# One more row block gathered in the first layer, one-hots made two batches ahead, idle products in a shorter opening, and last matrices in another PSUM pool

## The chip, the core and the metric

The kernel runs on one core of a Trainium2 chip. The core has five engines with queues of their own: TensorE (PE, matrix products), VectorE (DVE), ScalarE (ACT), GpSimd (POOL) and SyncE (SP, which here only issues transfers). They go in step only through semaphores. The metric is the device time of one execution in microseconds, as the median of several runs.

## What is computed

A graph of 6250 nodes with 256 channels and 100000 edges goes through four layers. Each layer adds to every node the sum over its incoming edges and then runs a small network of three matrices:

```python
def agg(h):
    return jax.ops.segment_sum(h[src], dst, num_segments=N)
h = max(layernorm(x), 0)
for l in range(3):
    g = h + agg(h)
    g = relu(g @ W1s[l] + b1s[l]); g = relu(g @ W2s[l] + b2s[l]); h = g @ W3s[l] + b3s[l]
g = h + agg(h)
g = relu(g @ cW1 + cb1); g = relu(g @ cW2 + cb2)      # 64 channels
out = x + g @ cW3 + cb3
```

The edges come sorted by destination. All numbers are float32.

## The kernel before

The nodes are cut into 49 row blocks of 128 nodes. The first matrix of each layer is applied before the sum, so that a layer's input is kept in SBUF as `XY` (49 blocks, each with a high and a low part of 256 columns). For a row block the sum over edges is made in one of two ways.

- **By a product.** For the block an adjacency matrix of 128 columns by 49 x 128 rows with the counts of edges is built once, in the first layer, as bytes. A product with all of `XY` (49 matmuls of 128x512, line 1642 in the first layer, line 1720 in panels later) then gives the sums. The counts are cast to float on ACT or DVE (lines 1602 and 1618) ahead of the product.
- **By a gather.** POOL issues 17 indirect DMAs for the block (line 1427). Each brings 128 source rows into one of 24 buffers named `rows`. When the block's *visit* comes, PE sums those rows with one-hot matrices (line 1466, 46 matmul records in the trace) into `sums`, and DVE adds the result to the block's own row (`u`, lines 1486 and 1495).

In the first layer (called layer 0 in the code) 26 blocks are products and 23 are gathered. In the three layers behind it 20, 20 and 18 are gathered.

**Building the matrices** (`build`, lines 1092 to 1130) fills layer 0 beside the products. It goes in batches of four sub-lists of edges, and a batch is two *steps*. For a batch DVE makes two one-hot tensors, `lo` (`low_hot`) and `hi` (`high_hot`, both line 1073); each is a tile with two buffers. A step is two matmuls (line 1114) into a PSUM bank `bp`, and a copy to bytes into `at` (ACT in odd steps, line 1122, DVE in even ones, line 1124). Sixteen steps are one block. A finished block gets the identity added (line 1128) and is stored by SP (line 1129) for the later layers. 31 blocks are built in all, since five are wanted only later. The order of the blocks is the list `made`.

**The opening.** Nothing can be multiplied before the first matrix is there. So `PRE` = 12 open steps of the outer clock `now` run two build steps each with no product beside them. Then the products start.

**What sets the order.** Every instruction is recorded in one Python program, and each engine carries out its own in that order. The outer clock `now` counts units of four product matmuls. In each unit `tick` runs what is due (`later`, `job`), then some build steps run up to `goals`, then `prepare` casts counts three units ahead, and then come the products. A second clock, `clock`, adds a fixed cost for each piece of PE work (`passed`) and stands for PE's time. From it `Gathered` sets the rate of the gathers: `pace` is the layer's modelled time divided by the number of its gathers. Each gather waits for the PE instruction at which the modelled time reaches it (`after(got, ...)`), and a visit comes when the modelled time says that its rows are there.

**The three dense matrices** of finished blocks (`mlp`) run in two later pieces, `seconds` and `thirds`, in PSUM tiles `ps` of a pool of two banks, `ps_m`. The products of the later layers use a pool of four banks, `ps_a`, under the name `agg`. At the end of the last layer the last panel and block 48 run in a hurry through `mlp`.

Of the kernel before, what the change touches and what calls it, by code (L numbers as in the profile page):

```python
# [8 lines left out]
F32 = mybir.dt.float32  # L9
# [8 lines left out]
P = 128  # L18
# [378 lines left out]
def sorted_edges(  # L397
# [77 lines left out]

    teams = [(18, 2), (20, 4), (24, 4), (28, 4), (32, 4), (36, 4), (40, 2), (42, 2)]
    made = [b + i for b, n in teams for i in range(n)]
    for i in range(panels[-1][1]):
        made.insert((4, 9, 14, 19)[i], panels[-1][0] + i)
    made.insert(25, 17)  # L480
# [520 lines left out]
    with tc.manual_schedule():  # L1001
# [90 lines left out]
        def build(hots, ats, ps_b):  # L1092
# [3 lines left out]
            pair(hots, 0)  # L1096
            low_hot(hots, 0)
            high_hot(hots, 0)
            step = 0
            for k, (s, q0) in enumerate(batches):  # L1100
# [6 lines left out]
                for q in range(0, BATCH, 2):  # L1107
                    if q == 0:
                        low_hot(hots, k + 1)
                    elif q == 2:  # L1110
                        high_hot(hots, k + 1)
                    bp = ps_b.tile([P, W], F32, name="bp")
# [8 lines left out]
                    if step % 2 or step <= 2 * PRE:  # L1121
                        nc.scalar.copy(o, v)  # L1122
                    else:
                        nc.vector.tensor_copy(o, v)  # L1124
                    if half and q0 + q + 2 == GSUB:
                        p, i = place_of[b]
                        own = at[:, b, :]
                        nc.vector.tensor_tensor(own, own, ident, OP.add)
                        nc.sync.dma_start(out=mats[p][:, :, i, :],
                                          in_=at.rearrange("p (k h) d -> p k (h d)", h=CH))  # L1130
# [66 lines left out]

        used, kept, wanted, lent = set(), set(), [], [0, 0]
        BACK = 3

# [49 lines left out]
        def mlp(l, b0, n, h1, hurry, far):  # L1250
# [7 lines left out]
            h2 = []  # L1258

            def second(i):  # L1260
                if i == 0:
                    h2.append(work.tile([P, KC, W], F32, name="h2"))
                ps = ps_m.tile([P, W], F32, name="ps")
                if twin:
# [17 lines left out]
            def halves():  # L1282
                m, w3 = n // 2, weights[l][1]
                pss = [ps_m.tile([P, W], F32, name="ps") for _ in range(2)]
                for q in range(m):
# [36 lines left out]
            def third(i):  # L1322
                m = min(2, n - i)
                w3 = weights[l][1]
                ps = ps_m.tile([P, W], F32, name="ps")
                for q in range(m):
# [32 lines left out]
            def seconds():  # L1359
                passed(BURST)  # L1360
                for i in range(-(-mid // P)):
                    second(i)
# [15 lines left out]
        class Gathered:  # L1378
# [30 lines left out]
            def begin(self):  # L1409
                self.one_hots(0)  # L1410
                self.end = begun[self.l] + work_of(self.l) - TAIL[self.l]
                self.pace = (self.end - clock[0] - MARGIN) / self.upto[-1]
                self.lead = MARGIN + self.upto[1] * self.pace
                self.first = clock[0] + self.lead
# [118 lines left out]

        EARLY = 8
        PRE = (GSUB + EARLY) // 2
# [130 lines left out]
        def product_of_team(b0, n, ps_a, beside, hurry):  # L1666
            us, h1 = [], []

            def turn(i, two):
                if not h1:  # L1670
                    h1.append(work.tile([P, KC, W], F32, name="h1", bufs=2) if hurry else
                              ats.tile([P, KC, W], F32, name="h1", bufs=1))
# [75 lines left out]
        with tc.tile_pool(name="hots", bufs=1) as hots, tc.tile_pool(  # L1748
# [9 lines left out]
            layers[0].send(8)  # L1758
            beside = build(hots, ats, ps_b)
            while now[0] < PRE:  # L1760
                for _ in range(2):
                    next(beside)
                    built[0] += 1
                tick(layers[0])
                layers[0].advance()
# [77 lines left out]
```

## Time and profile before

| | us |
|---|---|
| median of 3 runs | 2105.08 (2103.89 to 2105.66) |
| the profiled execution's own time | 2104.15 |
| its span, first to last instruction | 2102.4 |
| first build matmul | 116.58 |
| first product | 128.34 |
| last visit of layer 0 begins | 670.07 |
| first product of the next layer | 688.08 |
| PE busy | 2031.7 (97%) |
| POOL busy | 1441.1 (69%) |
| DVE busy | 933.8 (44%) |
| ACT busy | 879.7 (42%) |

Times inside the execution are counted from the span's start. In a row of the timeline stand the start, the length, the engine, the source line, the operation, the tile written and those read, and in brackets the idle time ahead of it with what ended that. "x4" is the number of instructions in the row. In a row of groups the number behind the bar is the busy time and the mean of one in nanoseconds. Matmuls overlap in the records: a row's length is longer than its distance to the next row, so rates of PE are read from start to start.

### The profile page before, as it was taken

The numbers are of one execution on the slowest core, as the hardware profiler recorded it, in microseconds if no ns is written. First come the engines' busy times: TensorE is split into PE (matmuls) and PEld (weight loads), VectorE is DVE, ScalarE is ACT, GpSimd is POOL, SyncE is SP. The second block draws the span as 40 slices with busy tenths as digits, with TensorE's granted clock in tenths as the row PEclk, the third lists the DMA queues.
The fourth block names the chain that finished last, engine by engine and source line by source line (L and its number), as shares of the span: only waits on it lengthen the run. The fifth ranks groups of instructions, "written<-read, shape, count | busy, mean of one in ns | idle before, by whom it ended". The sixth has DMA issues, their size and how long they took to land. (4 is left out here: it accounts for less than half of the span.)

```text
span 2102.4 us, 33308 instructions
## 1 busy us (share of the span) xinstructions
PE 2031.7 (97%) x12117; PEld 1501.4 (71%) x12117; DVE 933.8 (44%) x2108; ACT 879.7 (42%) x1799; POOL 1441.1 (69%) x1450
## 2 busy tenths in 40 slices
PE   6889999999999999999999999999999999999997
PEld 4667666666667777777777777777777777777775
DVE  5987767767673422222233322222224333333333
ACT  5866656556555523322333432323333433323331
POOL 3747777777774377777777377777777377777773
PEclk9999999999999999999999999999999999999999
DMA  5544545545554654545556555555456455656554
GB/s 166 171 136 137 158 150 154 157 150 153 155 153 145 212 163 146 169 152 179 155 174 196 186 165 149 172 159 179 147 171 202 161 179 156 196 174 206 169 171 129
DMA packets 184324, 346.92 MB, mean 165 GB/s; under 512 B 32030, under 2 KB 118080, under 8 KB 184150
## 3 DMA queue, kind: packets, MB, share of 16 engines
q0 software_dynamic: 68144, 183.13, 29.9%
q1 hardware_dynamic: 114078, 159.72, 23.1%
q8 instruction: 97, 1.59, 0.3%
q10 hardware_dynamic: 1928, 1.85, 0.3%
q14 instruction: 77, 0.63, 0.1%
HBM read 286.50 MB, written 58.07 MB: 164 GB/s over the span
## 5 line engine op out<-in xcount | busy, mean ns | idle before, releaser
L1427 POOL DMA_INDIRECT rows<-table,idx x1377 | 1381.2, 1003 | 587.5 <-issue 225.4
L1720 PE MATMUL agg<-a,XY 128*128 128x512 f32 x4116 | 976.6, 394 | 1.9 <-DVE clT L1654 1.9
L1720 PEld LDWEIGHTS agg<-a,XY 128*128 128x128 f32 x4116 | 765.2, 188 | 190.1 <-issue 32.4
L1618 ACT CAST a<-at 128x512 fp32r<-128x512 uint8 (+1 forms) x549 | 332.7, 616 | 633.2 <-PE agg L1720 591.3
L1618 DVE CAST a<-at 128x512 fp32r<-128x512 uint8 (+1 forms) x550 | 251.0, 458 | 522.4 <-PE agg L1720 476.0
L1642 PE MATMUL agg<-XY,a 128*128 128x512 f32 x1519 | 420.9, 410 | 1.7 <-ACT a L1602 1.0
L1642 PEld LDWEIGHTS agg<-XY,a 128*128 128x128 f32 x1519 | 268.3, 189 | 54.2 <-issue 9.2
L1466 PE MATMUL sums<-rows,hot 128*32 128x256 f32 x3726 | 233.4, 381 | 8.7 <-DMA rows<-table,idx 8.5
L1122 ACT CAST at<-bp 128x392 uint8<-128x392 f32 x260 | 125.0, 489 | 188.8 <-PE bp L1114 182.6
L1466 PEld LDWEIGHTS sums<-rows,hot 128*32 128x32 f32 x3726 | 118.5, 109 | 117.1 <-issue 27.6
L1602 ACT CAST a<-at 128x512 fp32r<-128x512 uint8 (+2 forms) x362 | 197.5, 575 | 4.7 <-PE agg L1642 4.7
L1124 DVE CAST at<-bp 128x392 uint8<-128x392 f32 x236 | 132.8, 563 | 133.5 <-PE bp L1114 132.7
L1495 DVE TENSOR_TENSOR u<-u,sums 128x256 f32<-128x256 f32 x81 | 33.9, 419 | 265.3 <-PE agg L1720 241.9
L1114 PE MATMUL bp<-hi,lo 128*128 128x196 bf16 x992 | 129.5, 251 | 16.9 <-DVE hi L1073 16.1
L1073 DVE TENSOR_TENSOR hi<-cols,pairs 128x784 bf16<-128x784 bf16 x248 | 139.1, 561 | 0.0
L1333 PE MATMUL ps<-w,h 128*128 128x256 f32 x588 | 135.1, 382 | 1.4 <-ACT h L1279 0.9
L1276 PE MATMUL ps<-h,w 128*128 128x512 f32 (+3 forms) x332 | 133.7, 545 | 2.0 <-DVE zz L1317 1.7
L1114 PEld LDWEIGHTS <-lo 128*128 128x128 bf16 x992 | 72.8, 98 | 87.7 <-DVE hi L1073 37.3
L1333 PEld LDWEIGHTS ps<-w,h 128*128 128x128 f32 x588 | 112.4, 192 | 18.7 <-ACT h L1279 1.3
L1073 DVE TENSOR_TENSOR lo<-lanes,pairs 128x512 bf16<-128x512 bf16 x248 | 103.6, 418 | 0.2 <-issue 0.2
L1530 ACT ACTIVATE h<-ps,bias 128x256 f32<-128x256 f32 (+1 forms) x116 | 47.5, 464 | 134.1 <-PE ps L1526 134.1
L1341 DVE TENSOR_TENSOR zz<-ps,w 128x512 f32<-128x512 f32 (+1 forms) x75 | 50.2, 678 | 117.1 <-PE ps L1333 117.1
(173 smaller groups left out, 959.0 us busy)
## 6 DMA issues: line engine op xcount, KB each, us to landing
at<-mat SPq DMA_DIRECT2D x152, 448.0 KB
mat<-at SPq DMA_DIRECT2D x31, 784.0 KB
rows<-table,idx POOLq DMA_INDIRECT x1377
table<-zz SPq DMA_DIRECT2D x72, 256.0 KB
back<-table SPq DMA_DIRECT2D x99, 128.0 KB
xs<-in_x_dram SPq DMA_DIRECT2D x8, 768.0 KB
table<-zs SPq DMA_DIRECT2D x12, 512.0 KB
out_dram<-zz SPq DMA_DIRECT2D x24, 256.0 KB
```

Of the source, the lines that this page charges most:

```text
L1073: nc.vector.tensor_tensor(o.rearrange("p q (n t) -> p q n t", t=2), values.rearrange("p (n t) -> p n t", t=2)[:, None, :, :].to_broadcast( ...
L1114: mm = nc.tensor.matmul(bp[:, m * HW:(m + 1) * HW], lo[:, q + m, :], hi[:, q + m, :], start=True, stop=True)
L1122: nc.scalar.copy(o, v)
L1124: nc.vector.tensor_copy(o, v)
L1276: mm = nc.tensor.matmul(ps[:mp, :w], weights[l][0][:, c, i * P:i * P + mp], h1[:, c, :w], start=(c == 0), stop=(c == KC - 1))
L1333: mm = nc.tensor.matmul(o, h2[0][:, c, nodes], w3[:, c, :], start=(c == 0), stop=(c == KC - 1))
L1427: got = nc.gpsimd.indirect_dma_start(out=t, out_offset=None, in_=tables[self.l][:, :], in_offset=bass.IndirectOffsetOnAxis(ap=idx[:, o:o + ...
L1466: nc.tensor.matmul(self.sums[m * Q:(m + 1) * Q, :C], self.hot[:, c - min(rounds), m, :], self.rows[g, c + 4 * m], start=(c == ROUNDS[0][0] ...
L1602: nc.scalar.copy(a[:, i * m * P:(i + 1) * m * P].rearrange("p (j d) -> p j d", j=m), counts[b][:, j:j + m, :])
L1618: cast(o, at[:, :, d:d + m * P])
L1642: mm = nc.tensor.matmul(agg, a[:, d:d + P], XY[:, j, :], start=(j == 0), stop=(j == NT - 1))
L1720: mm = nc.tensor.matmul(agg[c][:, :w], XY[:, j, o:o + P], a[:, :w], start=(at == 0 and half == 0), stop=(at == NT - 1 and half == 1))
```

## The change

1. The first team of layer 0 is block 19 alone in place of 18 and 19. Block 18 is gathered in layer 0, so that 24 blocks are gathered and 25 multiplied. Its matrix is still built, later, for the last layer. The group that it joins goes through the dense matrices with three blocks, and block 19 with one.
2. `lo` and `hi` of batch k + 2 are made behind the second step of batch k. Before, `lo` of batch k + 1 was made at the first step of batch k and `hi` at the second. The two buffers of each stay.
3. `EARLY` falls from 8 to 4, so `PRE` from 12 to 10. In each open step PE also runs two 128x512 products whose result nobody reads (`still`). The one-hot for the first visit moves from the start to the fourth unit behind the opening.
4. A set `held` keeps a team's first turn into `h1` (one buffer in layer 0) until the team ahead has begun its second matrix.
5. The matrices of the last panel and of block 48 take banks of `ps_a` in place of `ps_m`.

```diff
-    teams = [(18, 2), (20, 4), (24, 4), (28, 4), (32, 4), (36, 4), (40, 2), (42, 2)]
+    teams = [(19, 1), (20, 4), (24, 4), (28, 4), (32, 4), (36, 4), (40, 2), (42, 2)]
...
-        made.insert((4, 9, 14, 19)[i], panels[-1][0] + i)
+        made.insert((4, 8, 12, 17)[i], panels[-1][0] + i)
+    made.insert(21, 18)
     made.insert(25, 17)
...
             pair(hots, 0)
-            low_hot(hots, 0)
-            high_hot(hots, 0)
+            for k in range(2):
+                low_hot(hots, k)
+                high_hot(hots, k)
...
                 for q in range(0, BATCH, 2):
-                    if q == 0:
-                        low_hot(hots, k + 1)
-                    elif q == 2:
-                        high_hot(hots, k + 1)
                     bp = ps_b.tile([P, W], F32, name="bp")
...
                         nc.vector.tensor_copy(o, v)
+                    if q + 2 == BATCH:
+                        low_hot(hots, k + 2)
+                        high_hot(hots, k + 2)
                     if half and q0 + q + 2 == GSUB:
...
+            def bank():
+                return (ps_a.tile([P, W], F32, name="agg") if end and hurry else
+                        ps_m.tile([P, W], F32, name="ps"))
+
             def second(i):
...
-                ps = ps_m.tile([P, W], F32, name="ps")
+                ps = bank()
...
             def seconds():
                 passed(BURST)
+                if l == 0:
+                    held.discard(b0)
...
             def begin(self):
-                self.one_hots(0)
+                if self.l:
+                    self.one_hots(0)
+                else:
+                    later(PRE + 4, lambda: self.one_hots(0))
...
-        EARLY = 8
+        EARLY = 4
         PRE = (GSUB + EARLY) // 2
...
             def turn(i, two):
+                if not hurry and not h1 and held:
+                    job(1, 1, lambda: turn(i, two))
+                    return
                 if not h1:
+                    if not hurry:
+                        held.add(b0)
...
+            still = ps_m.tile([P, W], F32, name="ps")
             while now[0] < PRE:
                 for _ in range(2):
                     next(beside)
                     built[0] += 1
+                for _ in range(2):
+                    nc.tensor.matmul(still, XY[:, 1, :P], XY[:, 0, :], start=True, stop=True)
                 tick(layers[0])
```

How the change moves instructions is seen at three places. Lines of the changed file are larger by 1 to 16. The first is POOL's whole queue behind the preparation: the gathers of the four layers, from the tables 83 to 86. Before:

```order
L610 DMA near_i<-in_dst_dram,from_i 17x128
L610 DMA near_i<-in_src_dram,from_i 17x128
L1427 DMA rows<-table_83,idx 128x256 x391
L1427 DMA rows<-table_84,idx 128x256 x340
L1427 DMA rows<-table_85,idx 128x256 x340
L1427 DMA rows<-table_86,idx 128x256 x306
```

Now, in the same place:

```order
L611 DMA near_i<-in_dst_dram,from_i 17x128
L611 DMA near_i<-in_src_dram,from_i 17x128
L1438 DMA rows<-table_83,idx 128x256 x408
L1438 DMA rows<-table_84,idx 128x256 x340
L1438 DMA rows<-table_85,idx 128x256 x340
L1438 DMA rows<-table_86,idx 128x256 x306
```

Layer 0 issues 408 gathers in place of 391, and the other layers as many as before.

The second is DVE's queue in layer 0, at a unit in which two results of the third matrix (`zz`) are due. Before:

```order
L1124 CAST at<-bp 128x49x8
L1341 TENSOR_TENSOR zz<-ps,w_1173 128x512 x2
L1073 TENSOR_TENSOR lo<-lanes,pairs 128x512
L1073 TENSOR_TENSOR hi<-cols,pairs 128x784
L1124 CAST at<-bp 128x49x8
L1654 TENSOR_TENSOR un<-un,agg 128x256
```

Now:

```order
L1122 CAST at<-bp 128x49x8
L1074 TENSOR_TENSOR lo<-lanes,pairs 128x512
L1074 TENSOR_TENSOR hi<-cols,pairs 128x784
L1347 TENSOR_TENSOR zz<-ps,w_1173 128x512 x2
L1122 CAST at<-bp 128x49x8
```

The copy, `lo` and `hi` keep their order among themselves. What the unit has due besides stood between the copy and `lo`, and stands behind `hi` now.

The third is PE's queue at the opening, with buffer numbers: the end of the preparation, and the first batch. Before:

```order
L862 MATMUL ps_1138<-XY_71 128x512 x16
L1114 LDWEIGHTS lo_1217
L1114 MATMUL bp_1226<-hi_1219,lo_1217 128x196
...
L1114 MATMUL bp_1232<-hi_1219,lo_1217 128x196
...
L1114 LDWEIGHTS lo_1224
L1114 MATMUL bp_1238<-hi_1230,lo_1224 128x196
```

Now:

```order
L863 MATMUL ps_1138<-XY_71 128x512 x16
L1112 LDWEIGHTS lo_1216
L1112 MATMUL bp_1227<-hi_1218,lo_1216 128x196
...
L1112 MATMUL bp_1231<-hi_1218,lo_1216 128x196
L1782 MATMUL ps_1213<-XY_71 128x512 x2
L1112 LDWEIGHTS lo_1220
L1112 MATMUL bp_1241<-hi_1222,lo_1220 128x196
```

Rows that only repeat are left out of these two. Between batches of four build matmuls stand two products into one bank of `ps_m`. From the first product of the second layer to the end, PE's instructions are the same ones in the same order as before, but for the PSUM tiles of the last eleven.

More of the change, by code (lines that the diff above doesn't have):

```diff
@@ L1198, in sorted_edges @@
         used, kept, wanted, lent = set(), set(), [], [0, 0]
+        held = set()
         BACK = 3
@@ L1283, in halves @@
                 m, w3 = n // 2, weights[l][1]
-                pss = [ps_m.tile([P, W], F32, name="ps") for _ in range(2)]
+                pss = [bank() for _ in range(2)]
                 for q in range(m):
@@ L1324, in third @@
                 w3 = weights[l][1]
-                ps = ps_m.tile([P, W], F32, name="ps")
+                ps = bank()
                 for q in range(m):
```

## The prediction

> **What bounds the kernel now.** I read the page's shares first, then the stages, then in the first layer what PE waits for, and then POOL. The page gives each engine's busy time:
>
> ```profile
> PE 2031.7 (97%) x12117; PEld 1501.4 (71%) x12117; DVE 933.8 (44%) x2108; ACT 879.7 (42%) x1799; POOL 1441.1 (69%) x1450
> ```
>
> PE bounds the whole. The change lies in layer 0, so its stages come next (busy time of PE, weight loads, DVE, ACT, POOL with their counts, then granted clock and DMA):
>
> ```profile
> core 0: us, PE busy (x) PEld busy (x) DVE busy (x) ACT busy (x) POOL busy (x), PEclk, DMA share, GB/s
> 116.58:125.60 9.02, 5.20 (x41) 2.97 (x41) 8.48 (x22) 7.99 (x22) 7.19 (x7) 1.00 0.53 175
> 125.60:132.50 6.90, 5.87 (x22) 3.73 (x22) 3.74 (x11) 5.30 (x12) 1.22 (x2) 0.51 0.36 123
> 128.30:688.00 559.70, 544.32 (x3642) 384.17 (x3642) 381.77 (x868) 334.19 (x771) 387.34 (x383) 1.00 0.50 151
> ```
>
> The first row is the opening, where DVE and ACT are full and PE is not. In the second the clock is at half. The third is layer 0: PE is full, DVE at 68%. Its waits, by PE:
>
> ```profile
> PE bp L1114 <- DVE hi L1073: 11.7, 21, 1.2
> ```
>
> PE waits there for one thing, one-hots that come late. POOL's busy time hides a fixed gap behind each gather. Its group in layer 0 and in the third layer (busy, mean ns, idle ahead), and the gathers that begin and end a stage:
>
> ```profile
> L1427 POOL DMA_INDIRECT rows<-table,idx x383 | 387.3, 1011 | 152.7 <-issue 59.7 <-PE bp L1114 41.4 <-PE agg L1642 40.7
> ...
> L1427 POOL DMA_INDIRECT rows<-table,idx x340 | 337.6, 993 | 129.9 <-PE agg L1720 62.9 <-issue 56.1 <-PE ps L1333 3.7
> ...
> 137.12 0.95 POOL L1427 DMA_INDIRECT rows<-table,idx  x1 [9.99 <-PE agg L1642]
> ...
> 666.25 0.96 POOL L1427 DMA_INDIRECT rows<-table,idx  x1 [0.30 <-issue]
> ...
> 1634.79 0.95 POOL L1427 DMA_INDIRECT rows<-table,idx  x1 [0.30 <-issue]
> ```
>
> A gather takes 1.011 us here and at least 0.305 us passes to the next: a period of 1.316 us. The 382 periods from 137.12 to 666.25 need 502.7 of 529.1 us. So POOL is within 26.4 us (5%) of being a second bound of this layer. That is the number on which my forecast turns.
>
> **The opening (part 3).**
>
> ```profile
> 114.87 0.40 ACT L1068 COPY pairs<-clT 128x64 bf16<-128x64 bf16 x2 [1.74 <-DMA table<-zs]
> 116.95 3.33 ACT L1122 CAST at<-bp 128x392 uint8<-128x392 f32 x8 [1.68 <-PE bp L1114]
> ...
> 115.64 0.42 DVE L1073 TENSOR_TENSOR lo<-lanes,pairs 128x512 bf16<-128x512 bf16 x1
> ...
> 128.34 2.08 PE L1642 MATMUL agg<-XY,a 128*128 128x512 f32 x4 [1.03 <-ACT a L1602]
> 130.22 0.88 PE L1114 MATMUL bp<-hi,lo 128*128 128x196 bf16 x4
> 130.80 1.91 PE L1642 MATMUL agg<-XY,a 128*128 128x512 f32 x4
> 132.56 0.52 PE L1114 MATMUL bp<-hi,lo 128*128 128x196 bf16 x4
> ```
>
> The first product waits for ACT, which makes 24 copies at 3.33 / 8 = 0.41 us; four fewer give -1.6. Without the hot of the first visit ahead of it, `lo` waits only for `pairs` (114.87 + 0.40) in place of 115.64: -0.4. The first product comes at 126.3. Two idle products of 0.23 each (next part) and a batch fill about 0.8 us of PE per open step, as much as ACT's two copies take, so they cost nothing; were they the longer by 0.05, ten steps would lose 0.5.
>
> The clock: at half, two units of product ran from 128.34 to 132.56, 4.2 us; at full they take 0.9 + 1.3 = 2.2. If the idle products keep the clock up, -2.0. PE was busy 5.20 of 9.02 us before the drop, in pieces of half a microsecond with no long gap. The Trainium skill ("TensorE: Matmul & The Clock Gate", section "HAM oscillation — how this bites in real kernels") says that it is idle gaps above some 3.4 us that throttle. By that rule the opening was no cause, idle products change nothing, and the sum would end 2.0 higher. The row above shows 0.51 with no such gap, so I take -2.0.
>
> **One block from product to gather (part 1).**
>
> ```profile
> 185.55 2.09 PE L1642 MATMUL agg<-XY,a 128*128 128x512 f32 x8
> 187.49 0.51 PE L1114 MATMUL bp<-hi,lo 128*128 128x196 bf16 x4
> 187.78 1.17 PE L1642 MATMUL agg<-XY,a 128*128 128x512 f32 x4
> 188.79 0.52 PE L1114 MATMUL bp<-hi,lo 128*128 128x196 bf16 x4
> ...
> 201.62 2.80 PE L1466 MATMUL sums<-rows,hot 128*32 128x256 f32 x46
> 204.35 0.51 PE L1114 MATMUL bp<-hi,lo 128*128 128x196 bf16 x4
> ```
>
> Eight products take 0.92 longer than four, 0.23 each; 49 of them are -11.3. The visit is 204.35 - 201.62 = 2.7, with 0.1 to switch +2.8. The two batches that leave the opening come back here: a unit with a batch lasts 1.30 (187.49 to 188.79), without one 0.92, so +0.8. The dense matrices run over 384 + 128 columns in place of 256 + 256: 0. Together -7.7. On DVE a hot and two adds come and one add goes, on ACT 13 casts and a copy go; both lie beside PE. `held` (part 4) moves a turn by a unit: 0. SP stores 31 matrices as before; that of block 18 goes out later and is wanted first in the last layer: 0.
>
> PE alone would so end layer 0 at 688.08 - 2.0 - 2.0 - 7.7 = 676.4.
>
> **One-hots ahead (part 2).**
>
> ```profile
> 491.10 0.57 DVE L1124 CAST at<-bp 128x392 uint8<-128x392 f32 x1 [7.84 <-PE bp L1114]
> 491.58 1.28 DVE L1341 TENSOR_TENSOR zz<-ps,w 128x512 f32<-128x512 f32 x2
> 492.77 0.42 DVE L1073 TENSOR_TENSOR lo<-lanes,pairs 128x512 bf16<-128x512 bf16 x1
> 493.11 0.56 DVE L1073 TENSOR_TENSOR hi<-cols,pairs 128x784 bf16<-128x784 bf16 x1
> ...
> 493.72 0.51 PE L1114 MATMUL bp<-hi,lo 128*128 128x196 bf16 x4 [1.09 <-DVE hi L1073]
> ```
>
> Here 1.2 us of `zz` stood between the copy and `lo`, and PE waited 1.09. In the new order `lo` and `hi` come first. But then `zz` stands ahead of the next copy, whose `lo` and `hi` PE wants 1.3 us later. Copy, `lo` and `hi` start 0.48, 0.34 and about 0.47 apart, 1.29 against PE's 1.30, so the backlog only moves by a unit and goes where a unit has no batch. Those become fewer: 476 steps in 295 units against 472 in 308. The new wait of `lo` for batch k is one that the copy ahead of it has already had. Bounds: all 11.7 us go, or as many come. I take -4, since a third of the delayed units find a free one behind them; PE alone would then end at 672.4.
>
> **What POOL makes of it.** PE's gain calls for 408 gathers in less time. The first of those spaced by PE comes 4.0 earlier, at 133.1 (opening and clock). 399 periods of 1.316 are 525.1, and waits of some 0.5 remain: in the third layer idle time is 129.9 - 26.1 of its first wait = 103.8, which is 340 times 0.305, so there POOL waited for nothing. The last gather starts at 658.7. What a visit then costs, and what follows the last one, the timeline of PE shows:
>
> ```profile
> 1635.55 0.63 PE L1466 MATMUL sums<-rows,hot 128*32 128x256 f32 x6
> 1637.93 2.78 PE L1466 MATMUL sums<-rows,hot 128*32 128x256 f32 x40 [1.74 <-DMA rows<-table,idx]
> 1640.63 1.65 PE L1720 MATMUL agg<-a,XY 128*128 128x512 f32 x6
> ...
> 672.80 2.12 PE L1642 MATMUL agg<-XY,a 128*128 128x512 f32 x8
> ...
> 688.08 1.51 PE L1720 MATMUL agg<-a,XY 128*128 128x512 f32 x4 [1.85 <-DVE clT L1654]
> ```
>
> In the third layer PE was through with a starved visit 5.8 us after the gather (1634.79 to 1640.63). Behind layer 0's last visit the same instructions take 15.3 as before. So POOL ends the layer at 658.7 + 5.8 + 15.3 = 679.8, later than PE's 672.4 to 676.4: it is the bound, and the gain is 8.3, not 12 to 16. Ends: with the third layer's 0.993 the period is 1.298 and the end 672.6; with the opening's 7.19 / 7 = 1.027, where DVE is full, 1.332 and 686.2. I take the layer's own mean.
>
> **The tail (part 5).**
>
> ```profile
> 2088.39 1.28 DVE L1317 TENSOR_TENSOR zz<-ps,xt 128x512 f32<-128x512 f32 x2
> 2089.67 0.27 DVE L1304 MEMSET xt<- 128x256 f32 x1
> ...
> 2089.12 0.65 PE L1276 MATMUL ps<-h,w 128*64 128x128 f32 x4 [1.65 <-DVE zz L1317]
> ...
> 2090.87 2.23 DMA xt<-in_x_dram
> ```
>
> PE's wait of 1.65 for a bank goes. The chain of waits at the end runs through DVE's `zz`, the clearing of `xt` and its transfer instead, which no bank moves: 0 (between -0.6 and 0).
>
> **The sum.** 2104.15 of the profiled execution - 8.3 = 2095.9. The median is 0.9 above that execution, so 2097. With POOL's ends: 2089 to 2103.
>
> **Rivals.**
> - *POOL keeps up*, at 1.298 us or less. For it: the third layer does. Against it: DVE is at 68% in layer 0, 30% there. Then 672.6 or a little less: 2087 to 2092.
> - *The lookahead does not do what it says.* The denser steps bring back waits for one-hots, or gathers slow a little; layer 0 ends at 683 to 687: 2100 to 2104. For it: 1.29 against 1.30. Against it: late one-hots and late rows do not add, since DVE and POOL catch up while PE waits for the other.
> - *Slower: the gather's own time grows*, since no slack takes it up any more. At 400 gathers 0.01 us is 4 us. From a mean of 1.042 (period 1.347) the layer ends 4.2 us later than before, past 2109; at 1.06, 2117. For it: 1.027 in the opening; against it: no stage stands above that. The Trainium skill ("SBUF — State Buffer", section "Who interferes with whom") says that a DVE copy or cast in a two-port mode shuts GpSimd out for its whole length. By that rule the mean follows DVE's copies, which stay as many in 1.5% less time, and grows by 1.5% of what it has above the 0.95 of a single gather, less than 0.001. The trace agrees in sign: 1.011 at 68% DVE, 0.993 at 30%.
>
> **How the numbers follow.** The forecast has 0.54, POOL keeping up 0.23, the lost lookahead 0.14, the slower gather 0.09. Cases between 2089 and 2103 hold eight in ten: the forecast, most of the first rival and half of the second; the forecast's own range is 2093 to 2100. A difference below 0.2% (4.2 us) can't be told from none, so below 2100.9 is faster: the forecast, the first rival and 0.02 of the second, 0.79. The same: 0.12. Slower: 0.09.
>
> **What would show it.** After: first product near 126.3 with a clock of 1.00; first spaced gather near 133; gathers 0.305 apart almost without gaps, mean near 1.011; PE waiting at visits for rows in layer 0, where it never did; waits for `hi` below 11.7; the next layer's first product near 680, and from there the old distances. A gather mean off by 0.01, or clock drops from PE's new waits, would make the number wrong.

## The result, and the profile after

The changed kernel takes 2095.49 us (median of 5 runs, 2094.54 to 2096.54), beside 2105.08 for the kernel before (5 runs, 2103.89 to 2106.15): a ratio of 0.9956 (95% interval 0.9944 to 0.9969). The profiled execution took 2096.03 us and its span is 2094.2, 8.2 shorter than before's. The forecast was 2097.0 with a saving of 8.3, but the trace has the saving in another place. The shares of the page:

```profile
PE 2028.1 (97%) x12134; PEld 1499.2 (72%) x12134; DVE 932.0 (45%) x2112; ACT 876.2 (42%) x1786; POOL 1458.6 (70%) x1467
```

The stages, with the columns of the prediction (PE, weight loads, DVE, ACT, POOL, clock, DMA): the opening, the first units behind it, and layer 0.

```profile
116.58:126.00 9.42, 8.76 (x62) 5.82 (x61) 9.41 (x24) 8.87 (x23) 7.59 (x7) 1.00 0.53 174
126.00:133.00 7.00, 6.78 (x39) 5.08 (x40) 5.14 (x13) 6.25 (x14) 1.29 (x2) 1.00 0.39 128
126.20:687.60 561.40, 540.18 (x3648) 376.60 (x3648) 382.55 (x878) 329.09 (x762) 409.84 (x402) 1.00 0.52 156
```

The clock stays at 1.00 where it had been 0.51, and the first product comes at 126.22. But layer 0 is 561.4 us long, longer than before's 559.7. Its groups (busy, mean ns, idle ahead of it with what ended it):

```profile
L1438 POOL DMA_INDIRECT rows<-table,idx x402 | 410.7, 1022 | 130.9 <-issue 65.8 <-PE agg L1653 27.7 <-PE bp L1112 26.4
L1112 PE MATMUL bp<-hi,lo 128*128 128x196 bf16 x952 | 123.5, 250 | 9.4 <-DVE hi L1074 8.0
L1477 PE MATMUL sums<-rows,hot 128*32 128x256 f32 x1104 | 71.1, 386 | 6.7 <-DMA rows<-table,idx 6.7
```

The gathers have a mean of 1.022 us in place of 1.011. PE waits less for `hi`, and waits for rows at visits, which it never did in this layer. In the timeline: the first spaced gather and the last, one starved visit, the last visit, and the next layer's first product.

```profile
133.16 0.95 POOL L1438 DMA_INDIRECT rows<-table,idx  x1 [5.56 <-PE agg L1653]
665.69 0.95 POOL L1438 DMA_INDIRECT rows<-table,idx  x1 [0.30 <-issue]
...
622.31 0.63 PE L1477 MATMUL sums<-rows,hot 128*32 128x256 f32 x6
625.22 4.25 PE L1477 MATMUL sums<-rows,hot 128*32 128x256 f32 x40 [2.27 <-DMA rows<-table,idx]
629.40 0.68 PE L1112 MATMUL bp<-hi,lo 128*128 128x196 bf16 x4
...
669.40 2.80 PE L1477 MATMUL sums<-rows,hot 128*32 128x256 f32 x46
687.60 1.86 PE L1736 MATMUL agg<-a,XY 128*128 128x512 f32 x4 [2.00 <-ACT a L1629]
```

Four visits of layer 0 (from 303.31, 350.79, 598.81 and 622.31) take 10.4 us together above the 2.4 from first to last matmul that the others need. Layer 0 ends at 687.60, only 0.5 earlier than before. From one boundary to the next (the end of layer 0, and then the start of the last matmul in the last visit of layers 1, 2 and 3), the two traces differ as follows:

| | before | after | saved |
|---|---|---|---|
| to the end of layer 0 | 688.08 | 687.60 | 0.5 |
| layer 1 | 484.5 | 483.0 | 1.5 |
| layer 2 | 467.7 | 467.1 | 0.6 |
| layer 3 | 438.6 | 433.9 | 4.7 |
| behind the last visit | 23.5 | 22.6 | 0.9 |

Layer 3's largest saving shows in its groups, before and then after: the gathers are faster there, and PE waits less for rows.

```profile
L1427 POOL DMA_INDIRECT rows<-table,idx x306 | 307.9, 1006 | 131.4 <-issue 53.3 <-PE agg L1720 37.1 <-DMA w<-in_L_gnn_cW_dram 31.5
L1466 PE MATMUL sums<-rows,hot 128*32 128x256 f32 x828 | 53.2, 382 | 3.5 <-DMA rows<-table,idx 3.3
```

```profile
L1438 POOL DMA_INDIRECT rows<-table,idx x306 | 303.7, 992 | 130.6 <-issue 49.4 <-PE agg L1736 38.8 <-DMA w<-in_L_gnn_cW_dram 30.8
L1477 PE MATMUL sums<-rows,hot 128*32 128x256 f32 x829 | 51.6, 381 | 0.7 <-DMA rows<-table,idx 0.6
```

So two questions stand: why layer 0 kept nothing, and whether what layer 3 gave is the change's or chance.

### The profile page after: what moved, and what is told of

Same layout as the page of the kernel before. It is cut to its first block, busy times and chain, and to the rows that moved or that the text cites. A ratio compares the mean times of both kernels' runs of the same rounds, so it can differ in the third digit from the quotient of the medians.

```text
span 2094.2 us, 33375 instructions
## 1 busy us (share of the span) xinstructions
PE 2028.1 (97%) x12134; PEld 1499.2 (72%) x12134; DVE 932.0 (45%) x2112; ACT 876.2 (42%) x1786; POOL 1458.6 (70%) x1467
## 5 line engine op out<-in xcount | busy, mean ns | idle before, releaser
L1438 POOL DMA_INDIRECT rows<-table,idx x1394 | 1399.0, 1004 | 562.1 <-issue 230.1
L1653 PE MATMUL agg<-XY,a 128*128 128x512 f32 x1470 | 407.9, 409 | 1.4 <-DVE un L1665 0.7
L1653 PEld LDWEIGHTS agg<-XY,a 128*128 128x128 f32 x1470 | 258.1, 189 | 49.7 <-issue 7.2
L1477 PE MATMUL sums<-rows,hot 128*32 128x256 f32 x3772 | 237.0, 383 | 11.7 <-DMA rows<-table,idx 11.6
L1613 ACT CAST a<-at 128x512 fp32r<-128x512 uint8 (+2 forms) x349 | 190.8, 574 | 6.0 <-PE agg L1653 6.0
```

Source lines behind the costliest of these rows:

```text
L1438: got = nc.gpsimd.indirect_dma_start(out=t, out_offset=None, in_=tables[self.l][:, :], in_offset=bass.IndirectOffsetOnAxis(ap=idx[:, o:o + ...
L1477: nc.tensor.matmul(self.sums[m * Q:(m + 1) * Q, :C], self.hot[:, c - min(rounds), m, :], self.rows[g, c + 4 * m], start=(c == ROUNDS[0][0] ...
L1613: nc.scalar.copy(a[:, i * m * P:(i + 1) * m * P].rearrange("p (j d) -> p j d", j=m), counts[b][:, j:j + m, :])
L1653: mm = nc.tensor.matmul(agg, a[:, d:d + P], XY[:, j, :], start=(j == 0), stop=(j == NT - 1))
```

## What a gather waits for

A reading of both timelines came ahead of the experiments. A gather takes 0.953 us where nothing disturbs it. Of the 268 gathers before and the 291 after that took over 0.985 us, 254 and 274 end about 0.82 us behind the end of a DVE operation. The other 14 and 17 end 0.12 us behind a cast of counts that began some 0.44 to 0.64 us after them, and lose little by it, mostly 0.11 us or less. Here is one from layer 2 of the changed kernel:

```profile
1248.40 0.94 DVE L1461 TENSOR_TENSOR hot<-colf,rel 128x768 f32<-128x768 f32 x1
1248.54 1.63 POOL L1438 DMA_INDIRECT rows<-table,idx  x1 [0.30 <-issue]
```

`hot` had run for 0.14 us when the gather started. It ended at 1249.34, and the gather 0.83 later, at 1250.17. I sorted the gathers by the one DVE operation that was running at their start and for at least 0.135 us longer (the part of it that cost nothing), and left out gathers beside which a second operation started in that time. "Delayed" means that the gather's extra time is that operation's remaining time to within 0.03 us.

| operation running | inputs | delayed, before | delayed, after |
|---|---|---|---|
| `hot` | both in SBUF | 54 of 55 | 49 of 51 |
| `hi` (layer 0) | both in SBUF | 40 of 42 | 70 of 74 |
| `u<-XY` | both in SBUF | 16 of 17 | 19 of 21 |
| cast of counts `a<-at` | SBUF | 82 of 108 | 75 of 106 |
| copy `at<-bp` | PSUM | 0 of 80 | 0 of 50 |
| `u<-u,sums` | one in PSUM | 0 of 8 | 0 of 17 |
| `zz<-ps,w` | one in PSUM | 0 of 30 | 1 of 27 |

A gather's first 0.135 us are safe the other way too: operations that started within them cost nothing, with single exceptions. In layer 0 all delays together are 22.3 us over 383 gathers before and 27.5 over 400 after. Of these, the gathers in the table's row for `hi` make 9.2 and 17.4, since 74 of them stand there in place of 42.

This is what the Trainium skill says ("SBUF — State Buffer", section "Who interferes with whom"): a DVE instruction with two SBUF inputs contends with a GpSimd instruction that reads SBUF, and one with at most one SBUF input outside the two-port modes does not. The table agrees on both; why about a quarter of the casts delay nothing is open. The prediction had quoted only that section's part on copies and casts.

## Experiments

The theories are called A (the gain is made in layer 0 and kept), B (in the later layers the gathers meet DVE's operations at another phase, since the casts go to ACT and DVE in turn, unit by unit, and 13 units fewer, an odd number, swap the two), C (chance) and D (block 18 costs layer 0 more than it saves). Each ratio is to the kernel before, run on the same chip beside it.

### The block alone

```diff
-    teams = [(18, 2), (20, 4), (24, 4), ...
+    teams = [(19, 1), (20, 4), (24, 4), ...
...
+    made.insert(21, 18)
     made.insert(25, 17)
```

(with `held`)

> Before, with block 18 gathered in the first layer and with held, and nothing else of the change. Theory A (the change's gain is made in layer 0 and kept): PE alone would end layer 0 at 688.1 - 7.7 = 680.4; 399 periods of 1.316 us from 137.1 put the last gather at 662 to 665 and the end at 683 to 686, so layer 0 gives 2 to 5 us and the time is 2100 to 2103. Theory B (the gain of the changed kernel sits in the later layers, because 13 units fewer in layer 0 swap DVE's and ACT's casts there and so move DVE's operations against the gathers): the stretch from the end of layer 0 to the end of the last visit is 5 to 7 us shorter than before's 1390.8, and the time is 2094 to 2098. Theory C (that stretch varies by chance from one execution to the next): anything between, and the profile does not agree with the median.

2122.16 beside 2103.51: 1.0082 (1.0069 to 1.0095), slower. Layer 0 ends at 714.05, 26 us later than before. PE's wait at the build matmuls in layer 0, and the opening with its clock:

```profile
L1115 PE MATMUL bp<-hi,lo 128*128 128x196 bf16 x944 | 124.2, 252 | 34.9 <-DVE hi L1074 32.9 <-DVE at L1125 0.5 <-ACT at L1123 0.3
```

```profile
119.40:133.00 13.60, 11.04 (x49) 6.39 (x46) 9.66 (x25) 11.20 (x28) 6.34 (x6) 0.50 0.38 122
```

With 13 units fewer, the same build steps stand closer together, and with the old order of the one-hots the wait for `hi` nearly triples (before: 12.4 in all, 11.7 for `hi`). From its first product to its end the layer takes 25.4 us more (585.1 in place of 559.7): these waits are 22.5 of it, and three clock drops of 3.4 us at half in this layer some 5. The block takes away 8.5 of PE work (below), so some 6 stay open. A is refuted for this part. B's time is missed too, since B said nothing of layer 0; the stretch behind layer 0 took 1383.6 us, 7.2 less than before's and about what B gave, and layer 3 434.2 in place of 438.6.

### The one-hots alone

```diff
-                    if q == 0:
-                        low_hot(hots, k + 1)
-                    elif q == 2:
-                        high_hot(hots, k + 1)
...
+                    if q + 2 == BATCH:
+                        low_hot(hots, k + 2)
+                        high_hot(hots, k + 2)
```

> Before, with lo and hi made two batches ahead, and nothing else. A: waits for hi in layer 0 fall from 11.7 to about 8 us, POOL keeps its 23 blocks with slack, layer 0 ends at 684, time 2101. B: the same for layer 0; the later layers have the casts on the same engines as before, so their stretch of 1390.8 us stays within 1 us unless the phase alone moves it; time 2100 to 2102. Rival within B: if the phase of the gathers alone matters, the stretch moves by up to 5 us either way: 2096 to 2106.

2090.17: 0.9943 (0.9928 to 0.9958), no less than the whole change's gain, though its six runs lie between 2087.25 and 2095.70. All expectations missed: they had layer 0 end at 684 and the time at 2100 to 2102 (2096 to 2106 with the rival within B). Layer 0 ends at 675.50, 12.6 earlier. The wait, and the opening from the first build matmul on:

```profile
L1111 PE MATMUL bp<-hi,lo 128*128 128x196 bf16 x944 | 122.6, 250 | 4.2 <-DVE hi L1073 3.8 <-DVE at L1121 0.2
```

```profile
116.35:133.00 16.65, 12.02 (x82) 7.85 (x81) 14.77 (x38) 15.63 (x38) 8.58 (x8) 1.00 0.45 145
```

The idle time falls from 12.4 to 4.2 (8.2), the first product comes 1.0 earlier (127.31), and the 49 matmuls of the first block's product take 14.6 us in place of 16.5, since the clock does not drop. That is 11.1 of the 12.6. The last layer stays at 437.6.

### The opening alone

```diff
-        EARLY = 8
+        EARLY = 4
...
+                for _ in range(2):
+                    nc.tensor.matmul(still, XY[:, 1, :P], XY[:, 0, :], start=True, stop=True)
```

(with the later `hot`; the list `made` stays as before)

> Before, with the opening of ten steps, the two idle products in each and the later hot, and nothing else. A: first product near 126 in place of 128.3, clock 1.00 at once, so layer 0 ends 4 us earlier at 684, time 2101. Rival (the batches that leave the opening come back in layer 0 as late one-hots): layer 0 ends at 686 to 688, time 2103 to 2105. B says of the later layers what it says of one_hots: no swap of casts, the stretch stays near 1390.8.

2098.04 beside 2103.51: 0.9973 (0.9962 to 0.9983). Layer 0 ends at 684.27, 3.8 earlier, as A said; the rival (late one-hots) fails. The median is 3 below what A gave (the profiled execution itself took 2100.39), and this I do not explain.

### The tail alone

```diff
+            def bank():
+                return (ps_a.tile([P, W], F32, name="agg") if end and hurry else
+                        ps_m.tile([P, W], F32, name="ps"))
```

> Before, with the last matrices in banks of the panels' pool, and nothing else. The forecast: 0 to -0.6, time 2104.5 to 2105.1. What the trace after suggests: -0.3 from the last sums that wait for a bank, up to -0.9 with an earlier transfer of xt, 2104.2 to 2104.8. It also is a second profile of before up to the last panel, for its instructions are the same there: under C its layers end more than 2 us away from before's 688.1, 1195, 1665 and its last visit from 2078.9; under B they end within 1 us.

2103.65 beside 2103.51: 1.0002 (0.9993 to 1.0011), nothing. From the last visit to the end it takes 23.6 us, as before does. As a second profile of before it tells the scatter: its layer 0 ends at 689.6, and its layers take 481.9, 466.1 and 437.8, against 484.5, 467.7 and 438.6. So up to 2.6 us of one layer is chance (C): what layers 1 and 2 saved, 1.5 and 0.6, proves nothing. Layer 3 agrees to 0.8.

### The change without the block, and with the casts swapped

```diff
-    teams = [(19, 1), (20, 4), (24, 4), ...
+    teams = [(18, 2), (20, 4), (24, 4), ...
```

(and `made` as before), and in the second kernel also

```diff
-                cast = nc.scalar.copy if ready[0] % 2 else nc.vector.tensor_copy
+                cast = nc.vector.tensor_copy if ready[0] % 2 else nc.scalar.copy
```

> The changed kernel with block 18 as a product again (teams and the list made as before), all other parts kept. The forecast's theory (POOL bounds layer 0 and swallows what the block saves): about 2097 with it or without, within 1 us of the changed kernel. Theory D (the block's gather costs layer 0 more than its product: starved visits, late one-hots in denser steps, a clock drop): from one_hots' 675.5 and the opening's first product 1 us earlier, layer 0 ends at 673 to 676 in place of 687.6; the later layers need 1388 to 1391 as in before; time 2085 to 2090.

> As no_block, and DVE's and ACT's casts of the later layers swapped, as they are in the changed kernel. Theory B: the phase of DVE's operations against the gathers is what made the last layer shorter, so its stretch between last visits is 433 to 435 us in place of 437 to 439, and the time is 3 to 5 us below no_block. Theory C (chance): the same as no_block within 1 us.

2089.58, 0.9938 (0.9924 to 0.9952), and 2085.35, 0.9917 (0.9903 to 0.9932). Without the block, layer 0 ends at 675.87, 11.7 earlier than the changed kernel with it. PE waits for no rows there:

```profile
L1437 POOL DMA_INDIRECT rows<-table,idx x385 | 390.3, 1014 | 138.8 <-issue 66.7 <-PE bp L1111 35.4 <-PE agg L1652 27.6
L1111 PE MATMUL bp<-hi,lo 128*128 128x196 bf16 x952 | 123.2, 250 | 5.2 <-DVE hi L1073 3.7 <-ACT at L1119 0.3 <-DVE at L1121 0.3
L1476 PE MATMUL sums<-rows,hot 128*32 128x256 f32 x1058 | 64.3, 381 | 0.0
```

So D holds. From the first product to the end, the block makes layer 0 longer by 12.3 us (561.4 against 549.1). By the prediction's working it takes 8.5 us of PE work away (11.3 of products less 2.8 for the visit; the 0.8 that made 7.7 of it belongs to the shorter opening, which both kernels have). It brings 10.4 at starved visits, 4.2 at the build matmuls (9.4 against 5.2), and a clock drop of 3.4 us at half (1.7, behind the starved visit at 622). The remaining 4.5 no row names. In the whole time less of this shows (0.9938 against 0.9956), since without the block the casts lie as before again; with the swap put back it is 0.9917 against 0.9956, some 8 us.

The swap gives 4.2 us of median, and each run with it is below each run without. Layer 3, first without it, then with it:

```profile
L1437 POOL DMA_INDIRECT rows<-table,idx x306 | 307.5, 1005 | 130.4 <-issue 52.7 <-PE agg L1735 37.6 <-DMA w<-in_L_gnn_cW_dram 31.6
L1476 PE MATMUL sums<-rows,hot 128*32 128x256 f32 x844 | 54.4, 382 | 2.2 <-DMA rows<-table,idx 2.1
```

```profile
L1437 POOL DMA_INDIRECT rows<-table,idx x306 | 304.6, 995 | 129.9 <-issue 50.0 <-PE agg L1735 37.1 <-DMA w<-in_L_gnn_cW_dram 30.7
L1476 PE MATMUL sums<-rows,hot 128*32 128x256 f32 x838 | 52.7, 381 | 0.6 <-DMA rows<-table,idx 0.6
```

Over all traces in which `hot` has both inputs in SBUF, layer 3 takes 436.9 to 438.6 where the casts lie as before (before, tail, one_hots, opening, no_block) and 433.9 to 434.7 where they are swapped (after, one_block, no_block_swap, no_idle). The gathers that meet `hot` there lose 7.0 to 8.7 us in the first set and 3.7 to 4.0 in the second. Those that meet the casts themselves lose 3.0 to 3.9 and 3.7 to 4.1, so it is not the casts' own meetings that the swap saves. B holds for layer 3, and C is refuted there.

### Without the idle products

```diff
-                for _ in range(2):
-                    nc.tensor.matmul(still, XY[:, 1, :P], XY[:, 0, :], start=True, stop=True)
```

> The changed kernel without the idle products of the open steps. The forecast: the clock falls to half around the first products, and they lose 2.0 us: 2097.5. The Trainium skill's rule (TensorE: Matmul & The Clock Gate, section HAM oscillation): no gap of PE is above 3.4 us, so nothing changes: 2095.5. What one_hots suggests (12 open steps, no idle products, clock 1.00 throughout): the one-hots ahead alone keep the clock up, 2094.5 to 2095.5.

2093.03: 0.9954 (0.994 to 0.9968), the same ratio as with them. The clock does drop:

```profile
126.20:129.60 3.40, 3.40 (x15) 2.40 (x14) 1.57 (x5) 1.74 (x5) 0.95 (x1) 0.50 0.46 142
```

The first 49 products take 16.5 us in place of 14.9, so the mechanism of the forecast is there. The gain of the idle products does not reach the end: POOL sets it, and its last gather comes at 666.23, against 665.69 with them. Layer 0 even ends at 685.93 here, in place of 687.60. From the first build matmul to the first product it is 9.21 us without them and 9.46 with them.

### `hot` read against a PSUM operand

```diff
-                    colf.rearrange(...)
+                    (colp[0] if self.l else colf).rearrange(...)
...
+        colp.append(ps_c.tile([P, P], F32, name="colp"))
+        nc.scalar.copy(colp[0], colf)
```

> The changed kernel, with the column numbers that the one-hot of a visit (hot) is compared with lying in the free PSUM bank in layers 1 to 3. Theory B in its sharp form (a gather that reaches a certain moment, 0.135 us after its start, while DVE runs an operation that reads SBUF alone waits for its end; one that reads PSUM, as zz and at, delays none): the 45 gathers that now lose 18.7 us to hot in these layers lose less than 2, though hot itself may take up to twice as long; the gather mean falls from 1.002, 0.991 and 0.992 to 0.98, 0.97 and 0.98; the starved visits of these layers (8.7 us) fall below 4; time 2088 to 2092. Rival (the delay is any DVE operation's, or the memory's): hot lasts longer and so costs more, gather means the same or higher, 2095 to 2100.

2090.25: 0.9941 (0.9926 to 0.9955); no_idle (0.9954), which ran beside it on the same chip, is the nearest comparison: 2.8 us lower, with intervals that overlap, so the reading rests on the trace. The same gather as above, in this kernel:

```profile
1247.46 0.94 DVE L1462 TENSOR_TENSOR hot<-colp,rel 128x768 f32<-128x768 f32 x1
1247.60 0.96 POOL L1439 DMA_INDIRECT rows<-table,idx  x1 [0.31 <-issue]
```

`hot` had run for the same 0.14 us, and the gather takes 0.96 in place of 1.63. Layers 1 to 3, first the changed kernel, then this one:

```profile
L1438 POOL DMA_INDIRECT rows<-table,idx x986 | 981.2, 995 | 420.3 <-issue 162.7 <-PE agg L1736 143.4 <-DMA back<-table 46.1
L1477 PE MATMUL sums<-rows,hot 128*32 128x256 f32 x2668 | 165.9, 381 | 5.0 <-DMA rows<-table,idx 4.9
L1461 DVE TENSOR_TENSOR hot<-colf,rel 128x768 f32<-128x768 f32 x58 | 55.1, 949 | 0.0
```

```profile
L1439 POOL DMA_INDIRECT rows<-table,idx x986 | 964.7, 978 | 432.0 <-PE agg L1737 163.8 <-issue 160.7 <-DMA back<-table 44.4
L1478 PE MATMUL sums<-rows,hot 128*32 128x256 f32 x2668 | 164.5, 381 | 2.4 <-DMA rows<-table,idx 2.3
L1462 DVE TENSOR_TENSOR hot<-colp,rel 128x768 f32<-128x768 f32 x58 | 54.8, 945 | 0.0
```

Of 46 gathers that start during `hot` none is delayed to its end, and `hot` is no slower (0.945 against 0.949 us). Layer 2 takes 463.3 us in place of 467.1. The rival is refuted. The time is within what B gave (2088 to 2092); of the 8.6 us of long visits in these layers 4.7 stay, where B had less than 4.

### All three one-hots against PSUM operands

```diff
-                one_hot(lo, lanes, pairs[s]...
+                one_hot(lo, flat[1], pairs[s]...
...
+        for t, n in ((cols, HW // 2), (lanes, P // 2)):
+            nc.vector.tensor_copy(sums[:, at_word:at_word + n], t.bitcast(F32))
+            flat.append(sums[:, at_word:at_word + n].bitcast(BF16))
```

> The changed kernel with hot_from_psum's edit and, in layer 0, lo and hi compared with numbers that lie in the free half of the bank of sums. Theory B: the 144 gathers of layer 0 that lose 22 us to hi and lo lose less than 3, the gather mean there falls from 1.02 to 0.96 to 0.97, POOL has slack again, the starved visits of layer 0 (8.6 to 11.4 us so far) fall below 2, and the layer ends at 675 to 679 in place of 687.5; time 2078 to 2083. Rival 1 (an operand in PSUM makes lo and hi slower: their 0.42 and 0.56 us grow by half): DVE is full in layer 0, waits for hi grow, the layer ends past 690, time above 2092. Rival 2 (the block's gather costs layer 0 by late one-hots in denser steps, not by starved visits): gather mean falls, but the layer ends at 683 or later, time 2086 to 2090.

> no_block (18 a product, casts not swapped) with the same two edits as all_from_psum. Theory B: what the swap did to the last layer (437 to 434 us) was hot's collisions, so without any swap its stretch between last visits is now 433 to 435 and the starved visits of the later layers fall from 13.4 to 4 to 6 us; layer 0, which had no starved visit, still ends at 675 to 677; time 2079 to 2083. Rival: the swap did something else, the stretch stays at 437 and the time at 2083 to 2086. Between this and all_from_psum stands block 18 alone: if its price was POOL's (theory D in its form with starved visits), all_from_psum is now the same or faster; if not, it stays 5 to 10 us slower.

This pair ran on a chip on which the kernel before itself took 2342.23 us; all_from_psum took 2374.58, 1.014 (1.011 to 1.0169), and no_block_psum 2341.86, 1.0001 (0.9981 to 1.0022). PE's two largest waits in all_from_psum have no cause in the trace:

```profile
PE sums L1478 <- issue: 53.1, 104, 1.5
PE bp L1112 <- issue: 31.8, 27, 2.9
```

What slowed this chip is left open, and the pair was run once more.

> all_from_psum again: on the chip of the first try every kernel was 11% slower, the one before too (2342 us), with PE idle 53 us in its visits and 32 at the build matmuls for no cause that the trace names, so that only the gathers' own durations could be read (0.968 in layer 0, as theory B says, and hi at 0.55 us no slower, which ends rival 1). Where before takes about 2103 again: theory B 2078 to 2083, layer 0 ending at 675 to 679 with under 2 us of starved visits; rival 2 (the block costs by late one-hots) 2086 to 2090, layer 0 ending at 683 or later.

> no_block_psum again, beside all_from_psum_2. Theory B: last layer 433 to 435 us without a swap, starved visits of the later layers 4 to 6 us, time 2079 to 2083. Rival: the stretch stays at 437, time 2083 to 2086. And block 18 alone, all_from_psum_2 against this: the same or faster where its price was POOL's, 5 to 10 us slower where it was not.

2086.21, 0.9916 (0.9902 to 0.9929), and 2085.31, 0.9908 (0.9893 to 0.9923), beside 2104.43. Layer 0 of the first of them:

```profile
L1439 POOL DMA_INDIRECT rows<-table,idx x400 | 384.4, 961 | 151.6 <-issue 62.8 <-PE agg L1659 40.9 <-PE bp L1112 37.8
L1074 DVE TENSOR_TENSOR hi<-sums,pairs 128x784 bf16<-128x784 bf16 x236 | 130.4, 553 | 0.0
L1112 PE MATMUL bp<-hi,lo 128*128 128x196 bf16 x952 | 123.5, 250 | 9.0 <-DVE hi L1074 7.3
L1478 PE MATMUL sums<-rows,hot 128*32 128x256 f32 x1104 | 67.1, 381 | 6.0 <-DVE hi L1074 6.0
```

None of 79 gathers that start during `hi` is delayed, the mean falls from 1.022 to 0.961, `hi` is no slower, and no visit waits for rows. In their place stands a new wait of 6.0 us of the visits for `hi` (4.5 without the block): it reads the bank that the visit writes. The expectations had not foreseen this price of the edit, and with it layer 0 ends at 681.66 and 679.73, not at 675 to 679. With the waits for rows gone, the block costs 2.7 us of layer 0 (556.8 from first product to end, against 554.1) in place of 12.3, and the two medians are the same within their intervals. So most of the block's price was the delayed gathers. Without any swap, layer 3 of no_block_psum_2 takes 432.5 us (hot_from_psum, with it, 433.6): what the swap had done was `hot`'s meetings with gathers, as B said. Both medians came out 2 to 3 us above what theory B gave. That of all_from_psum_2 lies where rival 2 put it, but by waits for another cause, and that of no_block_psum_2 where its rival had it, but with the layer 3 that B gave.

The fastest kernels are no_block_psum_2 (0.9908), all_from_psum_2 (0.9916) and no_block_swap (0.9917), alike within their intervals and about twice as far below the kernel before as the changed kernel (0.9956).

## Why the prediction was right in the number, and wrong in the place

- **Opening: right, the first product in part by luck.** First product forecast 126.3, measured 126.22 at a clock of 1.00; the part alone ended layer 0 by 3.8 us earlier, forecast 4.0. But the term -0.4 did not come: the first build matmul stands at 116.76 in place of 116.58, since `pairs` was later. From there to the first product it took 9.46 us in place of 11.76, 2.3 less where the sum had 1.6: the opening alone gives 1.5 (10.23), and the one-hots alone 0.8 (10.96), which the sum did not have. The Trainium skill's rule that only gaps above some 3.4 us throttle ("TensorE: Matmul & The Clock Gate", section "HAM oscillation — how this bites in real kernels") would have left the clock as it was; the trace differs, since no_idle shows the drop with no gap above 1.23 us. But one_hots kept its clock without idle products, so they are not the only way.
- **One-hots: right in sign, mis-sized.** The term was -4 for the waits, and the part alone took 8.2 from them. The step that failed is "whose `lo` and `hi` PE wants 1.3 us later": what is made behind batch k is for batch k + 2, which starts two batches behind batch k, 2.6 us by the same row. That leaves time to make up most of what is late before PE asks, which fits the 8.2; no run takes it apart further.
- **The block: the step that failed.** The -7.7 was booked as PE's gain and POOL's limit applied to the sum, but never to the sum without the block. By the prediction's own numbers that sum is 672.4 + 8.5 = 680.9 (of the 7.7, 0.8 is the shorter opening's), with 17 gathers fewer, so against 679.8 the block was worth 1.1 at best. It cost 11.7: without it layer 0 ended at 675.9, 5.0 sooner than this sum, and with it 7.8 later than forecast (next point).
- **POOL as the bound of layer 0: right, mis-sized.** First spaced gather 133.16 (forecast 133.1), starved visits, gaps of 0.305. The last gather came at 665.69 in place of 658.7. 400 gathers longer by 0.011 are 4.4, and waits beyond the 0.305 between gathers, summed over the timeline, of 3.1 in place of 0.5 are 2.6. From there to the next layer it took 21.9 in place of 21.1. These are 7.8, all that layer 0 missed (687.6 for 679.8).
- **The gather's mean: the rival came half true.** The bound of that rival, 1.042, was not reached, but 1.022 took most of layer 0's gain. The estimate "less than 0.001" went by a count of copies. What counts is how many gathers start while `hi`, `lo` or `hot` runs, and the new order puts `lo` and `hi` together. one_hots has a mean of 1.023 in layer 0 and one_block, with the old order, 0.996; without the block (no_block, 1.014) it costs nothing, since POOL has slack there.
- **Tail: right alone (1.0002), but 0.9 in the changed kernel.** All kernels that have both the banks and the block take 22.5 to 22.7 us behind the last visit, and all others 23.2 to 23.6. Why the two act together is open.
- **"From there the old distances": failed.** PE's instructions stayed in order, but DVE and ACT swapped their casts, which the prediction did not look at. Layer 3 became 4.7 us shorter, and the kernels with swapped casts are 3.6 shorter there on average than those without.

The total was right by luck: layer 0 missed 7.8, and the layers behind it, the tail and chance gave 7.7 that was not forecast.

## What to carry to other kernels

When a change moves work from a full engine to one that is nearly full, make the sum with and without the move: the bound of the second engine can make the move worthless while the other parts look like its gain. Gathers from POOL are delayed by DVE operations with both inputs in SBUF that run at their start; one operand in PSUM took these delays away at no cost in DVE's time, but where PE also writes that operand's bank, PE waited 4.5 to 6.0 us for it in one layer. A change of parity or phase far upstream can be worth 0.2% by itself, so compare parts against kernels with the same phase.

## What the runs showed of the hardware that I had not expected

- **A gather's delay is nearly always all or nothing.** It is nothing or the running operation's remaining time, and can reach 1.2 us where `hot` follows `hi` without a break:

```profile
608.76 0.57 DVE L1074 TENSOR_TENSOR hi<-cols,pairs 128x784 bf16<-128x784 bf16 x1
608.86 2.16 POOL L1438 DMA_INDIRECT rows<-table,idx  x1 [0.30 <-issue]
609.24 0.96 DVE L1461 TENSOR_TENSOR hot<-colf,rel 128x768 f32<-128x768 f32 x1
```

The gather ended at 611.02, again 0.82 behind `hot`'s end. Of 11 gathers in the changed kernel that met `hi` with `hot` right behind it, three waited for `hot` too and the others got through at the end of `hi`; what decides this is open.

- **PSUM operands cost DVE nothing here:** `hot` 0.945 against 0.949 us, `hi` 0.553 against 0.557 to 0.564 in the traces with both inputs in SBUF.
- **The clock drops without a long gap.** Around the starved visit of the changed kernel (PE's busy time first, the clock third from the end):

```profile
600.00:622.30 22.30, 21.92 (x153) 16.22 (x153) 15.89 (x37) 14.58 (x34) 17.37 (x17) 1.00 0.53 158
622.30:626.40 4.10, 1.82 (x31) 0.92 (x33) 0.94 (x3) 0.00 (x0) 3.19 (x4) 1.00 0.58 170
626.40:629.80 3.40, 3.40 (x27) 1.47 (x20) 0.00 (x0) 0.00 (x0) 2.49 (x4) 0.50 0.32 94
```

PE's longest gap there was 2.27 us, and the next 3.4 us ran at half. Ahead of the drop in no_idle's opening, and in two stretches of the opening of one_hots, where no drop followed:

```profile
122.80:126.20 3.40, 1.87 (x14) 1.09 (x11) 2.34 (x7) 3.40 (x10) 2.56 (x3) 0.99 0.68 263
```

```profile
119.40:122.80 3.40, 2.09 (x16) 1.15 (x16) 3.40 (x10) 3.40 (x11) 2.79 (x3) 1.00 0.31 81
122.80:126.20 3.40, 2.21 (x18) 1.23 (x18) 3.40 (x10) 3.34 (x10) 2.49 (x4) 1.00 0.64 206
```

PE was busy for 55% of 3.4 us ahead of the drop, and for 61% and 65% where the clock stayed. But the share of busy time does not divide the cases. In a starved visit of hot_from_psum PE was busy for 45% of 3.4 us, and no drop followed:

```profile
304.10:307.50 3.40, 1.52 (x28) 0.97 (x32) 0.00 (x0) 0.00 (x0) 2.49 (x4) 1.00 0.66 204
307.50:310.90 3.40, 3.40 (x31) 2.25 (x24) 1.66 (x4) 1.52 (x4) 2.79 (x3) 1.00 0.40 116
```

Drops lasted 3.4, 6.8 or 13.7 us in these traces, but for the last of each, which runs into the kernel's end. Shown is that a drop needs no gap near 3.4 us; what decides it stays open.
